# Layer 2's projections moved into the end of layer 1's loop, by halves of 64 rows

## The chip, the core and the metric

The kernel runs on one core of a Trainium2 chip, from one program. The metric is the device time of one execution in microseconds (us), the median of the runs shown. A profiled execution of the same program gives the engine by engine picture. Engines: PE (TensorE) multiplies into PSUM, DVE (VectorE), ACT (ScalarE) and POOL (GpSimd) do the rest, SP issues most of the transfers. Each engine takes its instructions in the order of the program.

## The reference

Four graph layers over a batch of 8, 2048 nodes and 64 features, each with a residual and a layer norm. `adj` is a row-normalised adjacency matrix.

```python
x = layernorm(x + L0(x, adj))      # Chebyshev terms with weights per node
x = layernorm(x + L1(x, H, adj))   # hypergraph attention, mixed with (adj/deg) @ (x @ W_ind)
# layer 2
out_self = einsum('bni,io->bno', x, weight_self)
out_neighbors = einsum('bni,io->bno', einsum('nm,bmi->bni', adj, x), weight_neighbor)
x = layernorm(x + out_self + out_neighbors + bias)
# layer 3
x = layernorm(x + einsum('bnd,kd->bnk', einsum('bmd,nm->bnd', x, A_hat), W))
```

The change is about the two products of layer 2 with the 64 by 64 matrices `weight_self` and `weight_neighbor`, its **projections**.

## The kernel before, in words

The nodes lie in 16 tiles of 128 rows; a row holds all 8 batches of 64 features, 512 values in f32. `adj` is a 0/1 mask times a scale per row, so each product with `adj` is done as 16 row tiles of the mask (1 MB each, kept in DRAM) times a right-hand side that is split into a high and a low part (`y_hi`, `y_lo`), 32 matmuls of 128 by 512 for each output tile (`times_mask`, L1271).

**Layer 1** (`layer1`, L509) runs a loop of 19 iterations over 16 tiles, with several tiles in flight. `units(j)` makes the attention term g, `industry(j)` the product with the mask (`acc`, then `ind` and `dlt`, L774 and L778), `mix_and_norm(j)` the mixing and the layer norm, which ends with `x2[:, j]` (L855). The string `turns` (L868) is an order written out by hand: each entry names a generator and the step of it that comes next. In iteration t, `p` and `q` are the product of tiles t and t-1, `m`, `o` and `f` the mixer of tiles t-1, t-2 and t-3. So the last three iterations hold no product: in iteration 16 the last `ind` and `dlt`, the mixer of tile 15 up to `sw` and the norm of tile 14, in 17 the norm of tile 15, in 18 its x2. `program_order` (L195) ties the instructions of PE, DVE, ACT and POOL inside it to the order in which they are written.

Names in the mixer that matter here: `trm` are four transposes of g or ind into PSUM, `sT` their copy to memory on ACT (L805), `fc` four half matmuls (L813), `th` the tanh (L808, L816), the subtraction L818, `df` 8 products with one column (L822), `sw` (L828), then `mult`, `r`, `s`, `centre` on DVE (L830 to L839), `sq` on ACT (L844), `var` on DVE (L847), `rstd` on POOL (L849, L851), and x2 on ACT, 8 instructions (L855).

PSUM in the loop: `ps_g` (tag g) two banks in one buffer, `ps_m` two banks, `ps_s` one, `ps_acc` (tag acc, the product) one, `ps_fc` two: all eight. `small` tiles (sT, rstd and others) lie in the pool `fw`. A pool that is opened after layer 1 takes memory of the pools that layer 1 has closed. After layer 1 the pool `mj2` holds three mask tiles, `acc2` two PSUM banks for layer 2's products.

**Layer 2 before** comes after layer 1's pools are closed. For each tile (L1351 to L1372): `x_transposed` makes four transposes and a copy on DVE (L1347), then two times two matmuls of 128 rows by 256 columns with `w2_sb`, which holds two block-diagonal matrices of 128 by 128 (`block_diag`, L154), in PSUM tiles of one bank, two of them. Each half goes to u_hi on ACT (L1364), u_lo and x2 on DVE (L1365, L1368), and the bias is added on POOL (L1369). This part is outside `program_order`: the framework's scheduler sets its instructions among those of the first product. Then come the 16 products of layer 2 (L1398), each with its mask (L1399, issued by SP at L1268), r (L1404), a layer norm and layer 3's projection.

Of the kernel before, what the change touches and what calls it, by code (L numbers as in the profile page):

```python
# [8 lines left out]
F32 = mybir.dt.float32  # L9
# [9 lines left out]
P = 128  # L19
NT = N // P  # L20
# [26 lines left out]
def r_(ap):  # L47
    return ap.bitcast(F32R)
# [3 lines left out]
def kernel(  # L52
# [54 lines left out]
    def b_view(t2):  # L107
        return t2.rearrange("p (b c) -> p b c", b=B)
# [42 lines left out]
    def transpose(dst, src):  # L151
        nc.tensor.matmul(dst, src, ident, start=True, stop=True, is_transpose=True)  # L152

    def block_diag(dst, src):  # L154

        nc.gpsimd.memset(dst, 0.0)
        for h in range(2):
            nc.sync.dma_start(dst[h * 64:(h + 1) * 64, h * 64:(h + 1) * 64], src)
# [349 lines left out]
    @with_exitstack  # L508
    def layer1(  # L509
        stack, own, wts, fcw_sb, fcb_sb, av_sb, fcg_sb, vecs, pm, es, hgr, aggp, agg_st, h_sb,  # L510
        i_hi, i_lo, mask_tile, times_mask,
    ):


        l1 = stack.enter_context(tc.tile_pool(name="fl1", bufs=1))
# [268 lines left out]
        def mix_and_norm(j):  # L784
# [70 lines left out]
                nc.scalar.activation(x2[:, j, bc], r[:, bc], AF.Copy, scale=rstd[:, b:b + 1])  # L855
            yield "x2"

# [11 lines left out]
            "u.w1 m.df m.sw o.var"  # L872
        )

        def run(who, j, whats):
            for what in whats.split():
                if 0 <= j < NT:
                    got = next(who[j])
                    assert got == what, (j, got, what)

        with program_order():
            run(unit, 0, first)
            run(unit, 0, second)
            run(unit, 1, first)
            for t in range(NT + 3):
                now = {"p": (product, t), "q": (product, t - 1), "u": (unit, t + 1), "v": (unit, t + 2),
                       "s": (unit, t), "m": (mixer, t - 1), "o": (mixer, t - 2),
                       "f": (mixer, t - 3)}
                for turn_ in turns.split():
                    who, what = turn_.split(".")  # L890
                    run(*now[who], what)
        return x2


# [322 lines left out]
    def short_program(top):  # L1217
# [1 line left out]
        fcw_sb = wts.tile([P, J], F32, tag="fcw", name="fcw_sb")  # L1219
        fcb_sb = wts.tile([P, 1], F32, tag="fcb", name="fcb_sb")  # L1220
        av_sb = wts.tile([P, 1], F32, tag="av", name="av_sb")
        w2_sb = wts.tile([P, 2, P], F32, tag="w2", name="w2_sb")
        bias2_sb = wts.tile([P, C], F32, tag="bias2", name="bias2_sb")
        w3_sb = wts.tile([P, P], F32, tag="w3", name="w3_sb")

# [9 lines left out]
        def load_weights():  # L1235
            for h in range(2):
                s = slice(h * 64, (h + 1) * 64)
                nc.sync.dma_start(wb[s, 0:C], w1)
                nc.sync.dma_start(wb[s, C:2 * C], w1i)
            for i, v in enumerate((a_node, a_gn, a_ge)):  # L1240
                nc.sync.dma_start(vecs[:, i, :], v.partition_broadcast(P))
            nc.sync.dma_start(av_sb, av.rearrange("(f o) -> f o", o=1))
            block_diag(w2_sb[:, 0, :], w2s)
            block_diag(w2_sb[:, 1, :], w2n)
            nc.sync.dma_start(bias2_sb, bias2.partition_broadcast(P))
            block_diag(w3_sb, w3t)
            nc.gpsimd.memset(wa, 0.0)
            prod = wts.tile([P, C], F32, tag="prod", name="prod")
            for h in range(2):
                s = slice(h * 64, (h + 1) * 64)  # L1250
                for i in range(2):
                    nc.vector.tensor_tensor(prod[s], wb[s, 0:C], vecs[s, i, :], ALU.mult)
                    nc.vector.tensor_reduce(wa[s, i, h:h + 1], prod[s], AX.X, ALU.add)
# [30 lines left out]
        with tc.tile_pool(name="l0", bufs=1) as l0, tc.tile_pool(  # L1284
# [41 lines left out]

        x2 = layer1(
            own, wts, fcw_sb, fcb_sb, av_sb, fcg_sb, vecs, pm, es, hgr, aggp, agg_st, h_sb, y_hi,
            y_lo, mask_tile, times_mask,
        )  # L1330


        with tc.tile_pool(name="l2", bufs=2) as l2p, tc.tile_pool(
            name="mj2", bufs=3
        ) as mjp, tc.tile_pool(name="ylo", bufs=1) as ylop, tc.tile_pool(
            name="acc2", bufs=2, space=PSUM
        ) as ps_acc, tc.tile_pool(name="tr2", bufs=2, space=PSUM) as ps_tr, tc.tile_pool(
            name="mm2", bufs=2, space=PSUM
        ) as ps_mm:
            ln = ln_tiles(l2p)  # L1340

            def x_transposed(x, j, name):
                tr = ps_tr.tile([P, NP, P], F32, tag="tr", name=f"tr_{name}")
                for pr in range(NP):
                    transpose(tr[:, pr, :], x[:, j, pr * P:(pr + 1) * P])
                xT = l2p.tile([P, NP, P], F32, tag="xT", name=f"xT_{name}")
                nc.vector.tensor_copy(xT, tr)  # L1347
                return xT

            u_hi, u_lo = y_hi, y_lo  # L1350
            for j in range(NT):  # L1351
                xT = x_transposed(x2, j, f"l2_{j}")
                for p2 in range(2):
                    mm = ps_mm.tile([P, 2, 2, P], F32, tag="mm", name=f"u_{j}_{p2}")
                    for i in range(2):
                        nc.tensor.matmul(  # L1356
                            mm[:, i], xT[:, 2 * p2 + i, :], w2_sb, start=True, stop=True
                        )
                    cs = slice(p2 * 256, (p2 + 1) * 256)

                    def pair(t):
                        return t[:, j, cs].rearrange("p (i c) -> p i c", i=2)

                    nc.scalar.copy(r_(pair(u_hi)), mm[:, :, 1, :])  # L1364
                    nc.vector.tensor_tensor(  # L1365
                        r_(pair(u_lo)), mm[:, :, 1, :], pair(u_hi), ALU.subtract
                    )
                    nc.vector.tensor_tensor(pair(x2), mm[:, :, 0, :], pair(x2), ALU.add)  # L1368
                nc.gpsimd.tensor_tensor(  # L1369
                    b_view(x2[:, j, :]), b_view(x2[:, j, :]),  # L1370
                    bias2_sb.unsqueeze(1).to_broadcast([P, B, C]), ALU.add,
                )  # L1372


            v_hi = buffer(own, 0, "v_hi")
            v_lo01 = wts.tile([P, 2, BC], F32, tag="pm", name="v_lo01")
            v_lo = Tiles([v_lo01[:, t] for t in range(2)] + [
                ylop.tile([P, BC], F32, tag=f"b0_{t}", name=f"v_lo_{t}") for t in range(2, NT)
            ])

            def projected(j):
                xT = x_transposed(x2, j, f"l3_{j}")
                mm = ps_mm.tile([P, BC], F32, tag="mm", name=f"yp_{j}")
                for pr in range(NP):
                    nc.tensor.matmul(  # L1385
                        mm[:, pr * P:(pr + 1) * P], xT[:, pr, :], w3_sb, start=True, stop=True
                    )
                di = cols_of["dinv"][:, j:j + 1]
                nc.scalar.activation(r_(v_hi[:, j, :]), mm, AF.Copy, scale=di)
                nc.vector.scalar_tensor_tensor(  # L1390
                    r_(v_lo[:, j, :]), mm, di, v_hi[:, j, :], op0=ALU.mult, op1=ALU.subtract
                )
                nc.vector.scalar_tensor_tensor(
                    x2[:, j, :], mm, cols_of["dinv2"][:, j:j + 1], x2[:, j, :],
                    op0=ALU.mult, op1=ALU.add,
                )

            for j in range(NT):  # L1398
                a = mask_tile(mjp, j, "l2")  # L1399
                acc = ps_acc.tile([P, BC], F32, tag="acc", name=f"a2_{j}")  # L1400
                for mt in range(NT):
                    times_mask(acc, a, u_hi, u_lo, mt)
                r = l2p.tile([P, BC], F32, tag="r", name=f"r2_{j}")
                nc.vector.scalar_tensor_tensor(  # L1404
                    r, acc, cols_of["s1"][:, j:j + 1], x2[:, j, :], op0=ALU.mult, op1=ALU.add
                )
                layernorm(ln, r, x2[:, j, :], f"l2_{j}")
                if j:
                    projected(j - 1)
            projected(NT - 1)  # L1410
            for j in range(NT):
                a = mask_tile(mjp, j, "l3")
                acc = ps_acc.tile([P, BC], F32, tag="acc", name=f"a3_{j}")
                for mt in range(NT):
                    times_mask(acc, a, v_hi, v_lo, mt)
                r = l2p.tile([P, BC], F32, tag="r", name=f"r3_{j}")
                nc.vector.scalar_tensor_tensor(
                    r, acc, cols_of["sdinv"][:, j:j + 1], x2[:, j, :], op0=ALU.mult, op1=ALU.add
                )
                o = l2p.tile([P, BC], F32, tag="o", name=f"o_{j}")  # L1420
                layernorm(ln, r, o, f"l3_{j}")
                nc.scalar.dma_start(out[j * P:(j + 1) * P, :], o)
# [604 lines left out]
```

## Time and profile before

| | us |
|---|---|
| median of 3 runs | 1388.19 (1386.91 to 1389.96) |
| the profiled execution | 1406.12 |
| its span, first to last instruction | 1404.0 |
| PE busy in the span | 1323.9 (94%) |
| DVE busy | 931.5 (66%) |
| POOL busy | 444.2 (32%) |
| ACT busy | 364.1 (26%) |

The mean granted TensorE clock in that execution is 0.951 of full speed. The profiled execution is 17.9 us longer than the median of the runs; durations in the text come from it. Busy times add up what instructions took; the matmuls' ends are modelled. A line of a timeline gives the start in us from the span's start, the duration, the engine, the line of the source, the operation, output and inputs with their shapes and the count of instructions, and in brackets the idle time of the engine before it with what ended it. A matmul in f32 counts as two records here.

### The profile page before, as it was taken

What the parts mean: (1) busy time and instruction counts of PE and PEld (TensorE: products, weight loads), DVE (VectorE), ACT (ScalarE), POOL (GpSimd) and SP (SyncE); (2) the same over time, 40 slices, a digit from 0 to 9 for tenths busy, and PEclk for the clock granted to TensorE, in tenths of its full rate; (3) what the DMA queues carried; (4) which work ended last, traced back from release to release, by engine and by line L of the source; (5) the groups of instructions that cost most, each with busy time, mean ns of one, the idle gap of its engine ahead of it and who ended that gap; (6) DMA issues with size and microseconds to landing.
All of it is one profiled execution on the core that took longest, in us unless ns stands there. A gap on an engine that the chain in (4) does not pass through costs nothing.

```text
span 1404.0 us, 19827 instructions
## 1 busy us (share of the span) xinstructions
PE 1323.9 (94%) x7692; PEld 1033.8 (74%) x7692; DVE 931.5 (66%) x1658; ACT 364.1 (26%) x844; POOL 444.2 (32%) x373
## 2 busy tenths in 40 slices
PE   8999889999999999999977799999998799999997
PEld 6777678888888888888855466666666588888885
DVE  4555357787777777777753767678885666665554
ACT  3000101111111111111221345456665321111111
POOL 0000444444444444444201454546663420000000
PEclk9999999999999999999985788899999899999999
DMA  9865323333333333331504121222220213333551
GB/s 307 210 185 171 124 92 101 100 101 100 100 100 100 100 100 100 100 99 53 210 23 151 52 75 38 75 76 76 75 76 1 91 60 120 120 120 136 180 187 70
DMA packets 91047, 153.00 MB, mean 109 GB/s; under 512 B 12097, under 2 KB 55489, under 8 KB 84673
## 3 DMA queue, kind: packets, MB, share of 16 engines
q1 hardware_dynamic: 88642, 147.46, 31.6%
q10 hardware_dynamic: 2304, 4.20, 0.8%
q8 instruction: 63, 1.03, 0.3%
q14 instruction: 38, 0.31, 0.1%
HBM read 115.97 MB, written 35.66 MB: 108 GB/s over the span
## 4 chain that ended last, share of the span: by engine, by line
PE 91%; DVE 4%; issue 2%; ACT 1%; POOL 1%; DMA 1%; SPq 0%; ACTq 0%; DVEq 0%; POOLq 0%
PE pp L1035 23%; PE a L1273 17%; PE ind L1273 9%; PE y2p L998 9%; PE y1p L469 9%; PE fc L813 3%; PE u L1356 2%; PE df L822 2%; PE gp L708 2%; PE trm L152 1%; PE dp L733 1%; PE try L152 1%; PE aggp L1143 1%; PE hp L1113 1%; PE yp L1385 1%
## 5 line engine op out<-in xcount | busy, mean ns | idle before, releaser
L1046 DVE SCALAR_TENSOR_TENSOR r<-pp,emb_sb,r 128x256 f32<-128x256 f32 x512 | 247.3, 483 | 132.1 <-PE pp L1035 117.5
L1035 PE MATMUL pp<-w_sb,xT 64*128 64x256 f32 x1024 | 163.1, 391 | 11.9 <-PE hp L1113 10.3
L1035 PE MATMUL pp<-w_sb,y1T 64*128 64x256 f32 x1024 | 156.3, 377 | 0.0
L1035 PE MATMUL pp<-w_sb,y2T 64*128 64x256 f32 x1024 | 156.3, 377 | 0.0
L1035 PEld LDWEIGHTS pp<-w_sb,xT 64*128 64x128 f32 x1024 | 98.1, 188 | 35.1 <-issue 15.5
L749 POOL TENSOR_TENSOR ez<-ez,coef 128x1024 f32<-128x1024 f32 x32 | 65.0, 2032 | 153.9 <-DVE ez L747 131.4
L469 PE MATMUL y1p<-x_hi,m 128*128 128x512 f32 x256 | 107.0, 418 | 7.1 <-ACT x_hi L417 7.0
L1035 PEld LDWEIGHTS pp<-w_sb,y1T 64*128 64x128 f32 x1024 | 103.8, 188 | 7.7
L1035 PEld LDWEIGHTS pp<-w_sb,y2T 64*128 64x128 f32 x1024 | 103.8, 188 | 7.7
L1273 PE MATMUL ind<-y_hi,mj_l 128*128 128x512 f32 x256 | 107.1, 418 | 0.7 <-DVE dlt L778 0.7
L998 PE MATMUL y2p<-y_hi,msk 128*128 128x512 f32 x256 | 103.8, 406 | 0.0
L1273 PE MATMUL a<-y_hi,mj_l 128*128 128x512 f32 x256 | 102.5, 401 | 0.0
L469 PE MATMUL y1p<-x_lo,m 128*128 128x512 f32 x256 | 102.3, 400 | 0.0
L998 PE MATMUL y2p<-y_lo,msk 128*128 128x512 f32 x256 | 102.0, 399 | 0.0
L1273 PE MATMUL a<-y_lo,mj_l 128*128 128x512 f32 x256 | 101.6, 397 | 0.0
L1273 PE MATMUL ind<-y_lo,mj_l 128*128 128x512 f32 x256 | 101.5, 396 | 0.0
L1273 PE MATMUL a<-v_hi,mj_l 128*128 128x512 f32 x256 | 100.5, 393 | 0.0
L1273 PE MATMUL a<-v_lo,mj_l 128*128 128x512 f32 x256 | 100.1, 392 | 0.0
L1138 POOL TENSOR_TENSOR hs<-h,es 128x512 f32<-128x512 f32 x16 | 16.7, 1042 | 237.6 <-DVE r L1046 195.4
L950 POOL TENSOR_TENSOR ms<-msk,srow 128x1024 f32<-128x1024 f32 x32 | 77.4, 2418 | 6.4 <-DVE ms L963 5.7
L1273 PEld LDWEIGHTS ind<-y_hi,mj_l 128*128 128x128 f32 x256 | 49.0, 192 | 34.2 <-issue 17.7
L971 POOL TENSOR_TENSOR y<-y_hi,y_lo 128x512 f32<-128x512 f32 x16 | 25.7, 1609 | 133.5 <-PE y1p L469 133.5
(262 smaller groups left out, 2499.2 us busy)
## 6 DMA issues: line engine op xcount, KB each, us to landing
mj_l<-mask SPq DMA_DIRECT2D x48, 1024.0 KB, 4.9
raw<-in_at SPq DMA_DIRECT2D x32, 512.0 KB, 4.8
adj<-in_at SPq DMA_DIRECT2D x64, 256.0 KB, 3.4
mask<-msk SPq DMA_DIRECT2D x32, 512.0 KB, 3.1
xraw<-in_xn SPq DMA_DIRECT2D x8, 512.0 KB, 5.6
oh<-oh SPq DMA_DIRECT2D x16, 256.0 KB, 3.8
xT<-in_xt SPq DMA_DIRECT2D x16, 256.0 KB, 3.0
xs<-in_xn SPq DMA_DIRECT2D x16, 256.0 KB, 2.7
```

Source lines behind the costliest of these rows:

```text
L152: nc.tensor.matmul(dst, src, ident, start=True, stop=True, is_transpose=True)
L469: nc.tensor.matmul(accs[q][jj], r_(m[:, t, jj * P:(jj + 1) * P]), r_(part[:, mt, :]), start=i + h + t == 0 and part is x_hi, stop=i == 3 a ...
L708: nc.tensor.matmul(gp[:, u, :], r_((oh01, oh23)[i][rs, cols]), r_(part[rs]), start=part is agg_hi, stop=part is agg_lo,)
L749: nc.gpsimd.tensor_tensor(by_b(ez), by_b(ez), per_b(coef, 2 * i, 2), ALU.mult)
L813: nc.tensor.matmul(fc[:, h, :], fcw_sb[rs], sT[rs], start=True, stop=True)
L822: nc.tensor.matmul(df[:, b:b + 1], th[:, b % 2, (b // 2) * P:(b // 2 + 1) * P], av_sb, start=True, stop=True,)
L950: nc.gpsimd.tensor_tensor(ms, m, srow[j].unsqueeze(1).to_broadcast([P, 8, P]), ALU.mult)
L998: nc.tensor.matmul(acc, r_(msk[j, mt // 8][:, mt % 8, :]), r_(part[:, mt, :]), start=mt == 0 and part is y_hi, stop=mt == NT - 1 and part ...
L1035: nc.tensor.matmul(pp[:, h, pl, :], terms[j][name][rs, 2 * bq + pl], w_sb[rs, k, dq * 4 * C:(dq + 1) * 4 * C], start=k == 0, stop=k == K - 1,)
L1046: nc.vector.scalar_tensor_tensor(rb, ppv[:, :, dd, :], emb_sb[:, j, d:d + 1], rb, op0=ALU.mult, op1=ALU.add)
L1273: nc.tensor.matmul(acc, r_(a[:, mt, :]), r_(part[:, mt, :]), start=mt == 0 and part is hi, stop=mt == NT - 1 and part is lo,)
L1356: nc.tensor.matmul(mm[:, i], xT[:, 2 * p2 + i, :], w2_sb, start=True, stop=True)
```

## The change

A generator `layer2(j)` inside `layer1` does the projections of one tile in two steps. Step one: four transposes of x2 into the PSUM home `acc`, and a copy to a tile under the tag sT, on ACT. Step two: 8 matmuls of 64 rows by 128 columns into the PSUM home `g`, each half of the rows in a bank of its own, against `w2_sb`, which now holds the neighbour's and the self weights side by side, for each half of the rows; then one copy of 512 columns for the high part on ACT, two DVE instructions of 512 columns (the sum into x2, the low part), and the bias on POOL. After the last `dlt` each turn with a valid tile calls for one step. What is left is run after the loop, still inside `program_order`. The loop that did the projections is taken out, and with it `block_diag` for w2.

```diff
+        def layer2(j):
+            tr = ps_acc.tile([P, BC], F32, tag="acc", name=f"tr2_{j}")
+            for pr in range(NP):
+                pc = slice(pr * P, (pr + 1) * P)
+                transpose(tr[:, pc], x2[:, j, pc])
+            xT = small("sT", f"xT2_{j}", (P, BC))
+            nc.scalar.copy(xT, tr)
+            yield
+            mm = ps_g.tile([P, 2, BC], F32, tag="g", name=f"u_{j}")
+            mm = mm.rearrange("p h (r c) -> p h r c", r=NP)
+            for pr in range(NP):
+                for h in range(2):
+                    rs = slice(h * 64, (h + 1) * 64)
+                    nc.tensor.matmul(
+                        mm[:, h, pr, :], xT[rs, pr * P:(pr + 1) * P], w2_sb[rs],
+                        start=True, stop=True,
+                    )
+            def by_half(t):
+                return t[:, j, :].rearrange("p (r h c) -> p h r c", h=2, c=C)
+            nc.scalar.copy(r_(by_half(i_hi)), mm[:, :, :, 0:C])
+            nc.vector.tensor_tensor(by_half(x2), mm[:, :, :, C:2 * C], by_half(x2), ALU.add)
+            nc.vector.tensor_tensor(
+                r_(by_half(i_lo)), mm[:, :, :, 0:C], by_half(i_hi), ALU.subtract
+            )
+            nc.gpsimd.tensor_tensor(
+                b_view(x2[:, j, :]), b_view(x2[:, j, :]),
+                bias2_sb.unsqueeze(1).to_broadcast([P, B, C]), ALU.add,
+            )
+            yield
...
+        def layer2_steps():
+            for j in range(NT):
+                while ("x2", j) not in done:
+                    yield
+                yield from layer2(j)
+        last = layer2_steps()
...
                     run(*now[who], what)
+                    if ("dlt", NT - 1) in done and 0 <= now[who][1] < NT:
+                        next(last, None)
+            for _ in last:
+                pass
...
-        w2_sb = wts.tile([P, 2, P], F32, tag="w2", name="w2_sb")
+        w2_sb = wts.tile([P, 2 * C], F32, tag="w2", name="w2_sb")
...
-            block_diag(w2_sb[:, 0, :], w2s)
-            block_diag(w2_sb[:, 1, :], w2n)
+            for h in range(2):
+                s = slice(h * 64, (h + 1) * 64)
+                nc.sync.dma_start(w2_sb[s, 0:C], w2n)
+                nc.sync.dma_start(w2_sb[s, C:2 * C], w2s)
...
-            for j in range(NT):
-                xT = x_transposed(x2, j, f"l2_{j}")
-                for p2 in range(2):
-                    mm = ps_mm.tile([P, 2, 2, P], F32, tag="mm", name=f"u_{j}_{p2}")
-                    for i in range(2):
-                        nc.tensor.matmul(
-                            mm[:, i], xT[:, 2 * p2 + i, :], w2_sb, start=True, stop=True
-                        )
...
```

More of the change, by code (lines that the diff above doesn't have):

```diff
@@ L510, in layer1 @@
         stack, own, wts, fcw_sb, fcb_sb, av_sb, fcg_sb, vecs, pm, es, hgr, aggp, agg_st, h_sb,
-        i_hi, i_lo, mask_tile, times_mask,
+        i_hi, i_lo, mask_tile, times_mask, w2_sb, bias2_sb,
     ):
@@ L873, in layer1 @@
         )
+        done = set()
         def run(who, j, whats):
@@ L879, in run @@
                     assert got == what, (j, got, what)
+                    done.add((what, j))
+        def layer2_steps():
[4 more added lines that the diff above has]
+        last = layer2_steps()
         with program_order():
@@ L1328, in short_program @@
             own, wts, fcw_sb, fcb_sb, av_sb, fcg_sb, vecs, pm, es, hgr, aggp, agg_st, h_sb, y_hi,
-            y_lo, mask_tile, times_mask,
+            y_lo, mask_tile, times_mask, w2_sb, bias2_sb,
         )
@@ L1348, in x_transposed @@
                 return xT
-            u_hi, u_lo = y_hi, y_lo
-            for j in range(NT):
-                xT = x_transposed(x2, j, f"l2_{j}")
-                for p2 in range(2):
-                    mm = ps_mm.tile([P, 2, 2, P], F32, tag="mm", name=f"u_{j}_{p2}")
-                    for i in range(2):
-                        nc.tensor.matmul(
-                            mm[:, i], xT[:, 2 * p2 + i, :], w2_sb, start=True, stop=True
-                        )
[L1359 to L1372, printed above, removed]
             v_hi = buffer(own, 0, "v_hi")
@@ L1401, in short_program @@
                 for mt in range(NT):
-                    times_mask(acc, a, u_hi, u_lo, mt)
+                    times_mask(acc, a, y_hi, y_lo, mt)
                 r = l2p.tile([P, BC], F32, tag="r", name=f"r2_{j}")
```

## The prediction

> **What bounds the kernel now.** I read the page first: PE is busy 94% of the span, and the chain that ended last is 91% PE, with `PE u L1356` (the projections to be moved) 2%. The change acts between the end of layer 1's last product and layer 2's first one, so I went on to the timeline of that stretch (start, duration, engine, line, what it does, idle time before it and its releaser):
>
> ```profile
> 1076.33 1.84 PE L822 MATMUL df<-av_sb,th 128*128 128x1 f32 x16
> ...
> 1078.99 0.75 DVE L778 SCALAR_TENSOR_TENSOR dlt<-ind,sdeg,g 128x512 f32<-128x512 f32 x1 [2.90 <-ACT ind L774]
> ...
> 1096.41 2.02 ACT L855 ACTIVATE x<-r,rstd 128x64 f32<-128x64 f32 x8 [2.90 <-POOL rstd L851]
> ...
> 1098.50 1.27 SPq L1268 DMA_DIRECT2D mj_l<-mask  x3
> ```
>
> The last `dlt` ends at 1079.7, the last x2 at 1098.4. PE is busy only 5.8 us between 1079 and 1097: there is the hole that the change wants to fill. The three masks for layer 2 are issued at 1098.50, and the DMA queue's own waits say what held the first:
>
> ```profile
> SPq L1268 <- PE fc L813: 38.0, 1, 38.0
> SPq L1268 <- ACT x L855: 14.4, 1, 14.4
> ```
>
> Those are the last readers of layer 1's small tiles (sT, rstd): the mask buffers lie on that memory and wait for all of it. Then the chain in order of time, inside the projections:
>
> ```profile
> 1135.40 1.73 PE u L1356 x8
> 1137.13 0.92 PE a L1273 x4
> 1138.05 1.73 PE u L1356 x8
> 1139.77 0.71 PE a L1273 x3
> 1140.48 0.88 PE u L1356 x4
> 1141.36 8.88 PE a L1273 x39
> ```
>
> Between the projections run the matmuls of layer 2's first product, a2_0. Its first consumer (r, L1404) starts at 1143.10, with all 32 matmuls done at about 1143.0. So the stage to be moved hides the mask load and the whole first product. **The yardstick is the end of a2_0: 1143.0 before.** After it both kernels do the same.
>
> **The TensorE clock.** Windows cut at the steps of the granted clock (length, PE busy, clock, DMA):
>
> ```profile
> 1061.14:1064.55 3.41, 2.59 (x20) 1.00 0.00 0
> 1064.55:1067.96 3.41, 3.41 (x11) 0.50 0.00 0
> 1078.20:1081.61 3.41, 2.18 (x12) 1.00 0.02 5
> 1085.03:1088.44 3.41, 1.90 (x16) 1.00 0.01 2
> 818.78:822.20 3.42, 3.42 (x12) 0.50 0.52 208
> ```
>
> After the window 1061.14 to 1064.55 (df, four transposes, a piece of fc) the clock falls to half, after 1085.03 to 1088.44 (df alone) again. 1078.20 to 1081.61 (fc 1.13 us, transposes 1.1 us) keeps it. 818.78 to 822.20 holds fc, transposes and small sx matmuls, looks 100% busy, and stays at half.
>
> **What the Trainium skill says.** (1) "TensorE: Matmul & The Clock Gate", Part 1, "What's actually happening": a free-running window of 3413 ns sets full or half clock. The trace agrees: steps at 1064.55, 1067.96 and 1088.44 lie one and six windows apart. (2) The same page, Part 4 "PE-mode transpose": transposes don't count as busy in the same way. The window at 818.78 agrees. (3) "TensorEngine Tiling (Array Packing)", "PSUM Bottleneck": tiling speeds up TensorE but not the eviction from PSUM. Here each projected tile still needs about 1.4 us of VectorE one after the other.
>
> **The change, part by part.** *Weights:* two of three 0.2 us memsets on POOL (at 0.9 to 3.1) go; four DMAs at 86.8 to 90.3 stay four. The first product's matmuls cover both: nothing; uncovered it would be under 1 us.
>
> *One tile in the new form.* Its 8 matmuls have the shape of hp (L1113), its transposes that of trx:
>
> ```profile
> 693.78 1.16 PE L1113 MATMUL hp<-wb,xT 64*128 64x128 f32 x16
> 733.37 2.08 PE L1113 MATMUL hp<-wb,xT 64*128 64x128 f32 x16
> 727.81 1.11 PE L152 MATMUL trx<-ident,x 128*128 128x128 f32 x4 [6.26 <-DVE x L1072]
> ```
>
> Full clock: 1.16 + 0.62 for transposes; half clock: 2.08 + 1.11. ACT: xT copy 0.59, hi copy 0.59 (L1130). DVE: add 0.69, subtract 0.69 (L1131); the xT copy of 0.68 leaves DVE. POOL: the bias add stays, 1.27 (L1369). The g home is single: the next tile's matmuls wait until add and subtract have read it. At half clock, during those 1.4 us, PE transposes the next tile and ACT copies it: 1.11 + 0.59 + gaps = 1.84. **Cycle: 2.08 + 1.84 = 3.92 us at half clock; 1.16 + 1.51 (evictions with gaps) = 2.67 at full.** Before, a tile took 2.77 at full clock with two a2_0 matmuls inside: the new form is no faster.
>
> *Its place.* The last dlt starts the steps: 21 in iteration 16, 8 in 17, 2 in 18, two per tile. So tile 14 ends ahead of the last x2, tile 15 after it. Every engine runs in order, so layer 1's instructions now queue behind waiting projections, and vice versa. First matmul set done: dlt 1079.7 + start and gaps 0.4 + 0.62 + 0.60 + 1.16 = 1082.6. I laid the four queues out with the rows' durations and 0.03 to 0.05 us a handover. What lengthens a cycle at half clock: trm(g) 1.1; sT and fc0 1.6; trm(ind) 0.5; sT again 0.1; th0 0.6; fc1 2.1; th1 with the subtraction 0.6; the 2.0 us of x2_13 on ACT 1.5; df15 3.6 (16 such matmuls at half clock take 3.57, L600); x2_14 1.5; for tile 15 the wait for var, rstd and x2_15, 2.7. Sum 16.1. Last matmuls: 1082.6 + 15 x 3.92 + 16.1 = **1157.5**.
>
> *Masks.* The last matmuls now read the last sT tile, so SP waits for them. The loads are the same three, behind a later event. Landing 4.9 us (median of L1268); the first `a` matmul before came 5.5 after the issue, perhaps for other reasons. I take 5.2 (bounds 0, if SP needn't wait, and 6): 1162.7. *a2_0 uncovered:* 32 matmuls, 0.227 us each at full clock, 0.43 at half (L1273 at 789 to 791). The projections before took 4.85 us (1097.25 to 1102.1) to get the full clock back: 4.85 + 21 x 0.227 = 9.6 (bounds 7.3 and 13.8). End **1172.3, 29.3 us later**. Against the profiled execution's 1406.1 that is 1435.4; the median of the runs is 1388.2, 0.987 of it, so +28.9: **1417**.
>
> *Why half clock.* From 1078.2 to 1081.6 PE now does four transposes and the first matmuls, 24% of that window, since trm(g) and fc0, which filled it before, queue behind. The trace lost its clock on 42% matmul and transpose work. Later windows hold transposes and 64-row matmuls with gaps, less than that at 818.78, which gave no clock back. Unknowns: draining between the array's 128-row and 64-row forms, twice a tile; in the row of 693.78 it doesn't show (0), and 0.2 us each would cost 6. POOL (26 us in the stretch) keeps up.
>
> **Rivals.** *Full clock throughout:* cycle 2.67, lengthening 14.0 in the same places: 1082.6 + 40.0 + 14.0 = 1136.6; + 5.2 + 9.6 = 1151.4, +8.4: **1396.5**. For it: the windows at 1078 and 1081 kept the clock on some 65% work. Against: the gap at the start. *Clock lost only about 1110,* in the windows with x2_13's stall and df15 (34%): 1146 + 14.8 = 1160.8, +17.8: **1406**. *Faster:* layer 1's rest falls into the gaps of the 2.67 us cycle and costs nothing: 1122.6 + 14.8 = 1137.4, -5.6 us: **1382.7**. It decides from the point where the last projection ends before 1128.2. For it: ACT has 10.8 and DVE 8.1 us of layer 1 left, less than the gaps' sum. Against: they come as blocks of 1 to 2 us in front of copies that PE waits for. *It doesn't do what it says:* masks that needn't wait would take off 5.2, no more, since a2_0's PSUM banks are the g home's, free only after the last subtraction; and if the steps came only after the loop, 16 cycles from 1098.4 would end at 1161, as in my forecast.
>
> **How the numbers follow.** A measurement can tell about 0.2% (2.8 us) from no change. Half clock nearly throughout 0.60 (1411 to 1427), lost midway 0.19, full clock 0.10, no change 0.03, faster 0.08. Hence slower 0.89, same 0.03, faster 0.08. From 1396 to 1426 about 0.18 is left out: faster, no change, half of the full-clock case's lower part, and a few dearer handovers.
>
> **What would show it.** Right: granted clock 0.5 from about 1082 to beyond 1160; the moved sets near 2.1 us; SP's first layer 2 mask issued just after the last of them; PE idle about 5 us, then 32 `a` matmuls on end; r (L1404) first at about 1172. The weakest step is the clock: sets of 1.16 us would put the result near 1397. A first r before 1143 would refute the whole account.

## The result and the profile after

The changed kernel takes **1401.61 us** (median of 3 runs, 1398.87 to 1403.11) against 1389.08 us for the kernel before on the same chip (4 runs, 1386.91 to 1390.23): ratio **1.0089, 95% interval 1.0063 to 1.0115**. Medians and ratios here leave out runs in a slower state at a lower granted clock, one each of this kernel (1425.8 us), `products_2`, `warm_gap` and `alt_homes`. It is slower, by 12.5 us (8.8 to 16.0 by the interval); the prediction had +28.9.

The profiled execution after took 1403.11 us, its span 1401.1 us, clock 0.955. That span is shorter than the one shown of before (1404.0), although the kernel is slower: in before's profiled execution the clock was at half for 44 us between the first and the last `dlt` of layer 1's loop, in after's for 10; the change doesn't touch that part. Before's last `dlt` started at 1078.99, after's at 1063.19. So I measure the stage from the start of the last `dlt` to the start of the first r of layer 2: **64.1 us before, 78.4 after, +14.3**. From there to layer 2's last r both profiles agree within 0.8 us, to the end of the span within 1.3.

The ends of that stage, in the timeline after (start, duration, engine, line, operation, idle time before it with its releaser):

```profile
1063.19 0.75 DVE L780 SCALAR_TENSOR_TENSOR dlt<-ind,sdeg,g 128x512 f32<-128x512 f32 x1 [2.90 <-ACT ind L776]
...
1120.72 2.02 ACT L857 ACTIVATE x<-r,rstd 128x64 f32<-128x64 f32 x8 [0.81 <-POOL rstd L853]
...
1126.19 1.27 SPq L1321 DMA_DIRECT2D mj_l<-mask  x3
...
1131.08 0.77 PE L1326 MATMUL a<-y_hi,mj_l 128*128 128x512 f32 x1 [5.05 <-DMA mj_l<-mask]
...
1141.56 0.75 DVE L1433 SCALAR_TENSOR_TENSOR r<-a,s,x 128x512 f32<-128x512 f32 x1 [13.58 <-PE a L1326]
```

The last x2 of layer 1, 17.4 us after the last `dlt` before, now comes 57.5 us after it: it queues among the projections. The masks are issued only after that. The DMA queue's own waits name what SP waited for, now a projection and no longer fc and x2:

```profile
SPq L1321 <- PE u L875: 95.8, 1, 95.8
```

And the chain in order of time has nothing beside anything else: transposes, copy, last projection, mask, then the whole first product in one piece.

```profile
1121.37 0.95 PE tr L152 x2
...
1122.32 0.97 PE tr L152 x2
...
1123.31 0.59 ACT xT L867
...
1123.94 2.10 PE u L875 x16
...
1126.19 4.75 DMA mj_l<-mask
1130.94 0.14 issue
1131.08 11.06 PE a L1326 x35
```

The last projection ends 62.1 us after the last `dlt`'s end. Before, with 26 of the 32 matmuls of layer 2's first product set among them, the projections ended 61.6 us after it, and the first r followed 1.7 us later. **The move into the hole brought the projections no earlier end, and uncovered 5.1 us of mask load and 10.5 us of product.**

### The profile page after: what moved, and what is told of

Read it like the earlier page. It is cut to its first block, busy times and chain, and to the rows that moved or that the text cites. A ratio compares the mean times of both kernels' runs of the same rounds, so it can differ in the third digit from the quotient of the medians.

```text
span 1401.1 us, 19983 instructions
## 1 busy us (share of the span) xinstructions
PE 1306.5 (93%) x7820; PEld 1024.1 (73%) x7820; DVE 920.8 (66%) x1610; ACT 369.4 (26%) x844; POOL 442.4 (32%) x371
## 4 chain that ended last, share of the span: by engine, by line
PE 79%; DVE 4%; ACT 2%; issue 2%; POOL 1%; DMA 0%; ACTq 0%; DVEq 0%; POOLq 0%; SPq 0%
PE pp L1085 23%; PE a L1326 17%; PE ind L1326 9%; PE y2p L1048 9%; PE fc L815 2%; PE df L824 2%; PE gp L710 2%; PE u L875 1%; PE try L152 1%; PE trm L152 1%; DVE r L1096 1%; PE yp L1414 1%; PE hp L1163 1%; PE aggp L1193 1%; PE red L760 1%
## 5 line engine op out<-in xcount | busy, mean ns | idle before, releaser
L1326 PEld LDWEIGHTS ind<-y_hi,mj_l 128*128 128x128 f32 x256 | 48.6, 190 | 33.7 <-issue 19.1
```

Source lines behind the costliest of these rows:

```text
L1326: nc.tensor.matmul(acc, r_(a[:, mt, :]), r_(part[:, mt, :]), start=mt == 0 and part is hi, stop=mt == NT - 1 and part is lo,)
```

## Experiments

Stage means: start of the last `dlt` to start of the first r, from each kernel's one profile. A cycle is the time from the start of one tile's projection matmuls to the start of the next tile's; it is bare where layer 1 doesn't lengthen it. A home is the PSUM buffer that a tile is given. Each ratio is to the kernel before on the same chip, and is not the quotient of the two medians.

### One half of the change each: the form alone, the place alone

`form_only` keeps the old place and loop, with 64-row matmuls, two homes of two banks and copies of 512 columns. `place_only` has the new place with 128-row matmuls against block-diagonal weights; the single home and the copies of 512 columns stay.

```diff
# form_only, in the loop of the kernel before
-   for p2 in range(2):
-       mm = ps_mm.tile([P, 2, 2, P], ...)      # 2 matmuls 128 x 256, copies of 256 columns
+   mm = ps_mm.tile([P, 2, BC], ...)            # 8 matmuls 64 x 128, copies of 512 columns
# place_only, in layer2(j)
-       nc.tensor.matmul(mm[:, h, pr, :], xT[rs, ...], w2_sb[rs], ...)
+       nc.tensor.matmul(mm[:, pr], xT[:, ...], w2_sb, ...)
```

> The kernel before, with its projections in the 64-row form but in their old place, after layer 1, in two PSUM homes of two banks, xT copy on DVE as before. Cover theory: the stage was bound by PE (39 us busy of 39); per tile 1.75 us of matmuls become 1.0 to 1.2, DVE's 2.1 us a tile and PE's with the first product (about 2.1) become the bound, 2.8 us a tile becomes 2.2 to 2.4: 5 to 8 us faster than before, 1382. Form theory: the form itself costs, 5 us or more slower than before.

> The changed kernel with the old form of the matmuls (4 of 128 rows by 256 columns against block-diagonal weights) in the new place and the new homes. Cover theory: the matmuls of a tile stand in a chain with one home, 1.75 us instead of 1.16, times 16 is 9 us more, less some half clock: 1405 to 1412, slower than the changed kernel. Form theory: the form was the loss, so the old one in the new place gives 1390 or less.

`form_only`: 1382.79 us (20 runs), ratio 0.9945 (0.9927 to 0.9963), stage 56.7. `place_only`: 1412.61 us (4 runs), ratio 1.0143 (1.0073 to 1.0214), stage 89.4. The two halves have opposite signs: in the old place the new form takes 7.4 us off the stage, the place adds 25.3 to the old form (21.7 to the new one). The timeline of `form_only`, DVE and PE:

```profile
1103.12 0.68 DVE L1368 TENSOR_TENSOR y_lo<-u,y_hi 128x512 fp32r<-128x512 f32 x1
1103.31 1.16 PE L1360 MATMUL u<-w_sb,xT_l 64*128 64x128 f32 x16
1103.72 0.68 DVE L1371 TENSOR_TENSOR x<-u,x 128x512 f32<-128x512 f32 x1
1104.32 0.68 DVE L1349 COPY xT_l<-tr_l 128x512 f32<-128x512 f32 x1
...
1107.20 0.40 PE L1275 MATMUL a<-y_lo,mj_l 128*128 128x512 f32 x1
1107.33 0.68 DVE L1368 TENSOR_TENSOR y_lo<-u,y_hi 128x512 fp32r<-128x512 f32 x1
```

Two tiles take 4.21 us (1103.12 to 1107.33), 2.1 us a tile against 2.77 in the kernel before. DVE is busy 3.77 us of that, PE, with the `a` matmuls of the product, 3.90. The form is a gain by itself; the place is the loss.

### Giving the cover back

`products_2` is the kernel after with layer 2's first two products set among the projections again.

```diff
+   catch_up(j - 2, 2)     # after each tile's step: 4 matmuls per row tile, for products 0 and 1,
+                          # in the two homes of ps_m, masks in buffers that layer 1 has left
```

> The kernel after, with layer 2's first two products set among the projections again: two mask tiles are loaded into the buffers of layer 1's mask pool that the last product has left, their PSUM homes are the two banks of ps_m, and 8 matmuls of the two products follow each tile's step, two tiles behind. Theory 'the loss is the cover that was taken away: 5.1 us of mask load and 10.5 us of the first product now lie bare': both are hidden again and the clock holds, since PE is over 60% busy: the first r about 68 us after the last dlt, the second r close behind it, total 1385 to 1389 (as before or a little faster), with about 3 us of waiting for the third product's mask, which still waits for the last projection. Rival 'the projections' own cycle is the loss': the added matmuls lengthen each cycle by what they take (1.8 us a tile) and the total stays at 1400 or above.

1389.26 us (19 runs), ratio 0.9989 (0.9967 to 1.0011): the whole loss is gone. It hides one product more than the kernel before did: the r of the third product comes 78.2 us after the last `dlt`, when the kernel after has its first. So the first r says little here; to layer 2's last r it is 191.4 us from the last `dlt`, 208.4 in the kernel after and 194.9 before (this profile is of the fastest of its runs, 1385.43). The cycle of a tile at full clock stayed 3.25 us (starts of u at 1098.06, 1101.32, 1104.57), with four `a` matmuls in it: there they cost nothing. In the first cycles that take them, with eight, it was 3.92 and 3.51. With them the clock also held until 1118.65, while it fell at 1096.17 in the kernel after; `warm_all` below shows what the clock alone is worth. What remains is the third product's mask:

```profile
1124.37 1.27 SPq L1350 DMA_DIRECT2D mj_l<-mask  x3
1129.37 0.76 PE L1355 MATMUL a<-y_hi,mj_l 128*128 128x512 f32 x1 [2.19 <-DMA mj_l<-mask]
```

### The mask wait by itself

`masks_early` moves the last small tiles to other pools, so that the mask memory is free after layer 1's last fc. `warm_gap` leaves the wait and fills it with 22 idle matmuls. `all_in` joins early masks and the two products.

```diff
# masks_early
-   xT = small("sT", f"xT2_{j}", (P, BC))
+   xT = row("g", f"xT2_{j}")
+   pool = wts if tag in ("sw", "s", "var", "rstd") else fw      # mhalf goes to wts too
# warm_gap, after the last step
+   for n in range(22): nc.tensor.matmul(spare, y_hi tile, y_hi tile, ...)
```

> The changed kernel, with what the end of layer 1 still reads (xT2, sw, s, var, rstd, mhalf) in other homes, so that the memory of layer 2's mask tiles is free after the last fc. Cover theory (the loss is the mask load and the first product, which the old projections hid): the three masks are issued some 40 us earlier, about 20 us after the last dlt; the 5.0 us of PE idle before the first product shrink to the 2 us until the last subtraction frees the PSUM home; 3 to 5 us off the changed kernel, 1398. Form theory (the 64-row matmuls and the half clock they run in are the loss): the first product begins no earlier in effect, within 1 us of 1402.

> The changed kernel with 22 matmuls of 128 by 512 after the last projection, into a PSUM tile that nobody reads, about 5 to 9 us of PE work in the wait for the first mask; they change no result. If the half clock after the idle wait matters, the first product takes 7.3 to 8.5 us instead of 10.5: 2 to 3 us faster than the changed kernel, 1399.5. If it doesn't, the same as the changed kernel, or later where the extra matmuls outlast the wait.

> The kernel with layer 2's first two products among the projections, and with layer 1's small late tiles in the pool of weights, so that the memory of layer 2's other mask buffers is free from layer 1's last fc on. In the kernel with the two products alone, the third product's mask was issued at 1124.37 and PE waited 2.2 us for it, with the clock at half for some us more. Theory 'mask cover': that wait goes, 2 to 4 us off: from the start of the last dlt to the last r 188 us (191.4 without the early masks, 208.4 in the kernel after), total 1385 to 1387. Rival 'the early masks cost as much in the loop as they bring', as the kernel after with early masks hinted: total 1389 to 1391.

`masks_early`: masks issued at 1087.61 instead of 1126.19, PE's idle time before the first `a` 2.21 instead of 5.05 us, stage 75.2 (3.2 less). The total, 1404.91 (4 runs, ratio 1.0102, 1.0031 to 1.0173), missed the forecast of 1398 and doesn't resolve that. `warm_gap`: stage 75.9, total 1401.60 (19 runs, ratio 1.0083, 1.0064 to 1.0101): the clock during the first product is worth 2.5 us in the profile, and no gain is resolved in the total. `all_in`: 1389.86 (22 runs), ratio 0.9976 (0.9961 to 0.9992), 191.1 us to the last r; as its rival said, no better than without the early masks. In its trace the mask wait is gone, but the last projection ended 63.9 instead of 61.2 us after the last `dlt`'s end, with the clock at half from 1100 to 1107.

### What bounds a projection's cycle

Two edits: odd tiles in fc's banks once the last tanh is done, or DVE's sum ahead of ACT's copy.

```diff
# alt_homes
+   if ("th1", NT - 1) in done and j % 2:
+       mm = ps_fc.tile([P, 2, BC], F32, tag="fc", name=f"u_{j}")
# add_first
+   nc.vector.tensor_tensor(by_half(x2), mm[..., C:2 * C], by_half(x2), ALU.add)
    nc.scalar.copy(r_(by_half(i_hi)), mm[..., 0:C])
-   nc.vector.tensor_tensor(by_half(x2), mm[..., C:2 * C], by_half(x2), ALU.add)
```

> The kernel after, but once layer 1's last tanh is done, the projections of tiles with odd numbers take the two banks of fc instead of those of g, so that two tiles are in flight. Theory 'the single home bounds the cycle once layer 1 is out of the way': the last 6 to 8 tiles go from 3.25 us a tile to about 2.4 (two DVE instructions at 0.69 with the wait for ACT's copy), 4 to 5 us off: stage from the last dlt to the first r about 74, total 1397. With it PE's busy share rises and the clock should hold. Rival 'ACT and DVE are the bound, or layer 1's rest is': cycle stays above 3.1, stage 77 to 79, total 1401 to 1403.

> The kernel after, with the sum into x2 on DVE written ahead of ACT's copy of the high part; both read the same PSUM home. In the kernel after, the sum started only when ACT's copy had ended, in all 16 tiles, and the full-clock cycle was 3.25 to 3.3 us, not the 2.67 of the prediction. Theory 'readers of one home go one after the other': the order of the two changes nothing (sum 0.69, copy 0.6, subtract 0.69 still in a row, and the subtract waits for the copy anyway): cycle 3.25, stage from the start of the last dlt to the first r 78 us, total 1402. Rival 'the wait was an accident of the order in the program, and the two may overlap': 0.6 us x 16 = 9 us less, stage 69, total 1393. Rival 'the clock decides': a shorter or longer cycle moves the busy share, so the stage may shift by whole windows of 3.4 us, without a change of the DVE to ACT order in the trace.

Neither came out faster than the kernel after: `alt_homes` 1407.28 (3 runs, ratio 1.0129, 1.0069 to 1.0188), stage 82.0, a total 5.7 us above it that the intervals don't tell apart; `add_first` 1412.78 (4 runs, 1.0173, 1.0126 to 1.022), stage 86.5, which is slower. The waits (us in total, times, longest) say that the two readers of one home follow one another in whichever order they are written. First the kernel after, then `add_first`:

```profile
DVE x L884 <- ACT y_hi L883: 33.3, 15, 5.5
```

```profile
ACT y_hi L884 <- DVE x L883: 39.2, 16, 3.2
```

But neither total measured the cycle. In both profiles the clock fell, at 1096 and 1098, and stayed at half for most of the rest. In `alt_homes` windows like these two kept it there (length, PE, PE loads, DVE, ACT, POOL busy, then clock):

```profile
1099.53:1102.94 3.41, 2.68 (x20) 2.05 (x18) 0.00 (x0) 0.67 (x2) 0.00 (x0) 0.50 0.00 0
1120.01:1123.42 3.41, 2.68 (x20) 2.08 (x18) 1.88 (x3) 0.87 (x2) 2.24 (x3) 0.50 0.00 0
```

At half clock PE is 79% busy and still doesn't get the clock back. So I ran both, and the kernel after, with idle matmuls that hold the clock.

### The same with the clock held

```diff
+   warm(8)     # ahead of the last tile's transposes
+   warm(4)     # ahead of each projection, once the last tanh is done
+   warm(22)    # in the mask wait
```

> The kernel after, with idle matmuls (128 by 512, result not used) on PE where it waits: 4 ahead of each tile's projection once layer 1's last tanh is done, 8 ahead of the last tile's transposes, 22 while the first mask comes. Theory 'what the stage lost beyond the bare mask load and first product is the granted clock, which falls in the windows with little work and comes back only after a nearly full one': the clock holds at 1.00 from the first tanh on, the cycles that took 4.2 us go to 3.3, the last tile's step loses 2.2 us, the first product goes from 10.5 to 7.8 us: the stage from the start of the last dlt to the first r falls from 78.4 to about 71 us, total about 1395. Rival 'PE isn't the bound there, so its clock costs only the first product's 2.7 us': stage 75 to 76, total 1399 to 1400. Rival 'the added matmuls are in the way': stage 80 or more.

> The same idle matmuls in the kernel whose odd tiles take the homes of fc. That kernel, without them, lost the clock from 1096 to 1141 and was 8 us slower than the kernel after, though its half-clock cycle was 3.85 us, the other's 4.2 to 4.3. Theory 'the single home bounds the full-clock cycle': with the clock held the cycle falls from 3.27 us to about 2.8 (PE has 0.66 + 1.16 + 0.92 us of work in it), 3 to 4 us less than warm_all in the stage: about 67, total 1391. Rival 'ACT and DVE, with layer 1's rest, bound it': stage as in warm_all. Rival 'two homes are slower in themselves': the total stays near 1410.

> The same idle matmuls in the kernel with DVE's sum ahead of ACT's copy, which without them was 10 us slower than the kernel after. Theory 'the order of the two makes no difference, since the second waits for the first either way, and the 10 us were clock (half from 1098 to 1125 in its profile)': with the clock held, cycle 3.3 us, stage 71 and total 1395, as warm_all. Rival 'the order itself costs 0.6 us a tile': total 1404 or more, and the cycle at full clock is near 3.9.

| kernel | runs | us | ratio (95%) | stage |
|---|---|---|---|---|
| warm_all | 20 | 1402.41 | 1.0075 (1.0056 to 1.0093) | 74.6 |
| alt_warm | 12 | 1404.08 | 1.0081 (1.0057 to 1.0105) | 76.2 |
| add_warm | 8 | 1406.60 | 1.0102 (1.0073 to 1.0131) | 78.4 |

`warm_all`: stage 3.8 less than after, of which 2.9 is the first product (7.6 us from the first `a` to r, 10.5 in after) and 1.0 the projections. Its forecast of 71 and 1395 missed; one stretch at half, from 1108 to 1114.9, remained after df, and the total doesn't show the 3.8 us (the profile is of the slowest of its runs, 1411.43, which lost its time ahead of the stage: its last `dlt` started at 1074.99). So most of the clock that was lost in the kernel after is worth some 4 us in the trace, not the 7.4 expected, and doesn't carry the result.

`alt_warm`: two homes do shorten the full-clock cycle, to 2.62 us:

```profile
1112.49 1.16 PE L891 MATMUL u<-w_sb,xT 64*128 64x128 f32 x16
1115.10 1.16 PE L891 MATMUL u<-w_sb,xT 64*128 64x128 f32 x16
1117.73 1.16 PE L891 MATMUL u<-w_sb,xT 64*128 64x128 f32 x16
```

The single home bounds the bare cycle, as its theory had it; but in all it gains nothing. Few cycles are bare, the last projection then waits longer for layer 1's last x2 (6.5 us between its start and that of the one before, 5.9 in `warm_all`), and this profile lost the clock early (1070 to 1081).

`add_warm`: its theory, that the order makes no difference, falls by the trace; the intervals of its total and that of `warm_all` overlap. The bare cycle is nearly the same (3.3 to 3.4 us), but, as I read it, the copy now stands 0.7 us later on ACT, and where a layer 1 block is queued behind it, that block is later too: cycles of 4.96 and 4.94 us around x2_13 and x2_14 against 4.23 in `warm_all`, and three others of 4.0 to 4.1 against 3.3. Five times 0.7 is 3.5 of the 3.8 us between the two stages. The further 6 us that `add_first` lost in its total I put down to the clock, at half from 1098 to 1125 in its trace; that isn't shown.

### A version that beats both

`form_free` is `form_only` with the small tiles in the pool of weights.

```diff
-   mhalf = l1.tile([P, B], F32, tag="mhalf", name="mhalf")
+   mhalf = wts.tile([P, B], F32, tag="mhalf", name="mhalf")
+   pool = wts if tag in ("sw", "s", "var", "rstd") else fw
```

> The kernel with the 64-row form in its old place, after layer 1's pools are closed, and with layer 1's small late tiles (xT2 is not there; mhalf, sw, s, var, rstd) in the pool of weights instead of those that layer 1 closes, so that the pools opened after it, masks and projections, wait for layer 1's last fc at most and no longer for the last x2. Theory 'in that place what is left to gain is the wait of the first projections and of the first mask for layer 1's last norm': the masks are issued about 10 us earlier, the first projections run in the hole that PE has from the last dlt on, stage 48 instead of 56.7, total 1375. Rival 'DVE, busy with layer 1's norms and 1.4 us a tile, fills the hole anyway': stage 55 to 57, total 1381 to 1384, that is the same as with the 64-row form alone.

**1380.83 us** (8 runs), ratio 0.9928 (0.9902 to 0.9953), stage 54.6 (from the slowest of its runs, 1386.23). The masks came 7.5 us after the last `dlt` started instead of 19.1, but the stage gained only 2.0. The rival had the size right; its reason, that DVE fills the hole, isn't in the trace: DVE is busy 20.2 of the 32 us from 1070 to 1102.

```profile
1081.96 3.50 PE L1361 MATMUL u<-w_sb,xT_l 64*128 64x128 f32 x32 [0.27 <-ACT sw L829]
...
1091.40 2.02 ACT L856 ACTIVATE x<-r,rstd 128x64 f32<-128x64 f32 x8 [3.71 <-POOL rstd L852]
...
1093.92 0.69 DVE L1369 TENSOR_TENSOR y_lo<-u,y_hi 128x512 fp32r<-128x512 f32 x1 [2.94 <-ACT y_hi L1368]
```

The first projection begins only when ACT's last `sw` is done, and the copies of the high part (1093.32) stand behind layer 1's last x2 on ACT, so DVE and then PE wait for it. From `form_only` the total isn't told apart. Both beat the kernel before and the changed one.

## Why the prediction was right and wrong

**Right: the yardstick, the direction and its cause.** The stage's change, +14.3, lies in the interval of the total's change, 8.8 to 16.0. What follows the first product moved by 1.3 us at most. SP waited for the last projection, and the mask load and the product lay bare. `products_2`, with one product more under cover than before, takes the loss back; holding the clock alone (`warm_all`) doesn't.

Of the forecast +29.3, 13.1 was load and product laid bare, measured 13.8; the other 16.2 was a later end of the projections, measured 0.5. **That second part was wrong.**

**Step by step**, in us from the last `dlt`'s end:

| step | forecast | measured after |
|---|---|---|
| last projection ends | 77.8 | 62.1 |
| mask to first `a` | 5.2 | 5.1 |
| first `a` to r | 9.6 | 10.5 |

**The step that failed is in the first row: "Half clock nearly throughout".** It needed two things. The clock was to fall in the window from the last `dlt` on, which it did. And "later windows hold transposes and 64-row matmuls with gaps, less than that at 818.78, which gave no clock back": that is false. Windows after, at the steps of the clock (columns as above):

```profile
1061.98:1065.40 3.42, 1.11 (x10) 0.79 (x9) 0.75 (x1) 1.34 (x3) 0.00 (x0) 1.00 0.00 0
1065.40:1068.81 3.41, 3.41 (x24) 3.19 (x24) 0.83 (x2) 0.59 (x1) 0.06 (x1) 0.51 0.00 0
1075.64:1079.05 3.41, 1.75 (x20) 1.42 (x20) 2.74 (x4) 1.55 (x3) 1.43 (x2) 1.00 0.00 0
...
1092.76:1096.17 3.41, 2.37 (x28) 2.25 (x28) 0.55 (x1) 2.10 (x6) 0.67 (x1) 1.00 0.00 0
...
1099.53:1102.94 3.41, 2.61 (x20) 1.99 (x16) 1.18 (x2) 1.17 (x2) 0.41 (x1) 0.50 0.00 0
1102.94:1106.36 3.42, 3.12 (x20) 2.53 (x20) 1.13 (x3) 0.58 (x1) 2.72 (x3) 0.50 0.00 0
...
1116.60:1120.01 3.41, 1.18 (x17) 1.00 (x16) 1.94 (x4) 1.23 (x3) 2.46 (x3) 1.00 0.00 0
```

1061.98 to 1065.40 is 32% busy: the clock falls. The next is all busy, with the first projection at 1.99 us and layer 1's transposes: one window, and the clock is back. The window at 1075.64 holds one projection (1.16 us) and its transposes, 51%: the clock stays. The one at 1116.60 holds the projection without transposes, 35%: it falls. So **transposes do count**, against what I took from the Trainium skill, "TensorE: Matmul & The Clock Gate", Part 4 "PE-mode transpose". The measurement decides. A line of the prediction could have said so: its window 1078.20 to 1081.61, with 1.13 us of fc (33%) and transposes beside it, kept the clock. The fall at 1096 follows a window with df: 1092.76 to 1096.17 is 69% busy by the records, with one projection and 1.3 us of df.

The projections then have, as I read it, **two modes: full clock keeps itself, half clock does in most windows**: with a 3.3 us cycle a window is about 51% busy, which keeps full clock; at half clock, with a cycle of about 4.2 us (after, 1099.01 to 1103.19), most windows are 75 to 79% busy, which doesn't bring it back, as at 1099.53 above and in `alt_homes`, at half for 44 us, but the windows fall differently on that cycle, and one of 91% (1102.94) did bring it back. My forecast is the second mode throughout. The profile after lies mostly in the first, since one full window early on switched it over, and that later one did so again. At half clock it spent some 20 of the 62 us. That was my rival "clock lost midway" (chance 0.19), which had +17.8 where the stage grew by 14.3; that it came so near was luck, since two errors in its time cancel.

**Those errors are the other terms of the sum.** The full-clock cycle, 2.67 in the prediction, measured 3.29 on the mean of the eight bare cycles at full clock: I took ACT's copy and DVE's two instructions as 1.51 us beside each other; they run one after the other, 0.58 + 0.69 + 0.68 us with handovers:

```profile
1077.50 0.58 ACT L883 CAST y_hi<-u 128x512 fp32r<-128x512 f32 x1 [2.02 <-PE u L875]
1077.98 0.59 ACT L807 COPY sT<-trm 128x512 f32<-128x512 f32 x1
1078.11 0.69 DVE L884 TENSOR_TENSOR x<-u,x 128x512 f32<-128x512 f32 x1 [0.67 <-ACT y_hi L883]
...
1078.72 0.68 DVE L885 TENSOR_TENSOR y_lo<-u,y_hi 128x512 fp32r<-128x512 f32 x1
1078.88 1.26 POOL L888 TENSOR_TENSOR x<-x,bias_sb 128x512 f32<-128x512 f32 x1 [1.98 <-DVE x L884]
1079.32 1.38 DVE L836 SCALAR_TENSOR_TENSOR r<-dlt,r 128x512 f32<-128x512 f32 x1
1079.55 1.16 PE L875 MATMUL u<-w_sb,xT 64*128 64x128 f32 x16 [1.50 <-DVE y_lo L885]
```

The sum at 1078.11 reads other columns than the copy at 1077.50 and waits for it all the same. The Trainium skill gives a reason in "PSUM — Partial Sum Buffer", "PSUM bank collisions raise a hardware error": two engines mustn't access one bank in the same partitions at once, two readers included, so the compiler sets them in a row. The runs show the wait, in both orders (33.3 and 39.2 us above), not its reason. The trace before showed it too (`dlt` on DVE waited for `ind` on ACT, both readers of the product's home), and I passed over it.

With the other sign, what layer 1 adds to the cycles was 16.1 (half clock; the terms listed there add up to 15.9) or 14.0 (full) in the prediction and 6.3 in the trace: trm(g) falls into the first cycle, at half clock, sT, trm(ind), fc and th cost nothing (their cycles are among the eight of 3.2 to 3.4), x2_13 0.9, df15 1.9, x2_14 0.9, tile 15 2.5. Three more cycles at half clock add 2.9 together. So 1065.33, the first start, + 15 x 3.29 + 6.3 + 2.9 = 1123.9, the start of the last. Counted from my full-clock sum, which had the last projection end 56.9 us after the last `dlt`'s end, the longer cycle adds 15 x 0.62 = 9.3, layer 1 takes 7.7 off, and 2.9 of half clock and a first set 0.5 later bring it to about the 62.1 measured. So the clock put 20.9 us into the forecast (77.8 against 56.9), and the two other errors nearly cancel.

**The faster rival** wanted the last projection to end before 1128.2, 48.5 us after the last `dlt`'s end. It came at 62.1; even in `warm_all` at 61.1. Its claim that layer 1's rest falls into the gaps was right for 8 of 15 cycles.

**Mis-sized on the other side:** the first product took 10.5 us instead of 9.6, at half clock until 1137.1.

**What stays open.** The medians of the kernel after and of its variants with idle matmuls or early masks don't resolve the 3 to 4 us that their profiles show; no run hid exactly one product in the new place, as the kernel before does in the old one; and the two modes of the clock are read from single profiles, so how often the kernel runs in each isn't known.

## What to carry to other kernels

A stage that fills a hole may itself be the cover of something: look at what runs between its instructions and what load waits for its last one, and price that uncovered before moving it. Judge form and place of a change apart; here one alone was 6.6 us faster and the other 23 us slower. When a stage's granted clock is in question, work out the busy share of its cycle at both clocks: if each clock can keep itself for a while, the forecast has two values, and single windows choose between them.

## What the runs showed of the hardware

- In the kernel after, the clock kept full rate with windows of 51% busy, transposes included, and lost it at 32 to 35%. Between these, `add_warm` kept it with 47% (1079.71 to 1083.12) and `products_2` lost it with 48% (1125.48 to 1128.89). From half it came back after windows of 91 and 100%, not after 76 to 79%. The recorded share is no exact measure: in `warm_all` the window from 1108.07 to 1111.48, all busy by the records, with the end of df in it, didn't bring it back.
- Windows with df (16 matmuls of one column) count for less than they look: the one at 1092.76 above, 69% busy, lost the clock, and so did the one in `warm_all` from 1104.65 to 1108.07, 72% busy by the records, again with one projection beside df.
- DVE's instruction at 1079.32 took 1.38 us beside POOL's bias add; the same line took 0.69 us in `add_warm` (at 1107.68). DVE's y_lo at 1078.72, beside the same add, took 0.68. The Trainium skill, "SBUF — State Buffer", "Who interferes with whom", says that a DVE instruction with two SBUF inputs contends with a GpSimd instruction that reads SBUF; this trace agrees, since y_lo has one input in PSUM. No experiment here took POOL's add away.
